# One-element additions that tie a graph layer's turning of finished rows to a later source tile

## Chip, cores and metric

The kernel runs on one NeuronCore of a Trainium2 chip. TensorE (PE in the profile) does matrix products and transposes, VectorE (DVE) and ScalarE (ACT) elementwise work, GpSimd (POOL) slower elementwise work and indirect transfers, SyncE (SP) issues transfers. Each engine works through its own list of instructions in a fixed order, and waits at an instruction until the semaphores that it names have been raised. The metric is the device time of one execution in microseconds; lower is better. Three runs of the kernel before took 1935.4, 1935.51 and 1937.74 us, so the median is 1935.51 us.

## What is computed

Four layers over 3125 nodes with 256 features: a three-layer graph attention network, an expert layer with 16 experts of which each node takes two, a graph sum layer, and an expert layer with 8 experts of which each node takes one. The change touches the first of these. Cut to it, the reference is:

```python
def _gat_layer(x, src, dst, W, al, ar, b, n_nodes):
    h = x @ W
    el = h @ al
    er = h @ ar
    e = jax.nn.leaky_relu(el[src] + er[dst], NEG_SLOPE)
    m = jax.ops.segment_max(e, dst, num_segments=n_nodes)
    ex = jnp.exp(e - m[dst])
    s = jax.ops.segment_sum(ex, dst, num_segments=n_nodes)
    alpha = ex / s[dst]
    out = jax.ops.segment_sum(alpha[:, None] * h[src], dst, num_segments=n_nodes)
    return out + b
...
h = jax.nn.relu(_gat_layer(x, src, dst, W1, al1, ar1, b1, n))
h = jax.nn.relu(_gat_layer(h, src, dst, W2, al2, ar2, b2, n))
h = _gat_layer(h, src, dst, W3, al3, ar3, b3, n)
```

There are 103,125 edges, loops included.

## The kernel before

The attention layers are computed densely. The kernel counts the edges between every pair of nodes once, during the first layer, into a matrix of small numbers (`counts`). A layer is then a product: for destination nodes d and source nodes s, the weight of s for d is a count times the larger of two exponential terms, and the sum over s is a matrix product on TensorE. With a column of ones scaled like the rest carried as column 257 of the source rows, the same product gives the softmax's denominator.

The work is tiled in 128 nodes: 25 tiles, the last with 53 nodes. Two destination tiles make a group, so that there are 13 groups, the last with one tile of 53. The loops are: three layers (`i`), in each 13 groups (`a`), in each 25 source tiles (`s`). For each group:

- line 1228: TensorE transposes the group's destination scores, and ACT (line 1230) makes `tau` of them;
- for each `s`, VectorE makes the factors `pm` (line 1247: the larger of `tau` and a source value, times the counts; six buffers), and TensorE multiplies them with the source rows (line 1250) into `acc`, a pair of PSUM banks, one for each tile of the group; each product in this precision is two passes on the array;
- when all 25 are summed, the group is finished in steps that are put in a list `later` and called at stated values of `s` of the next group.

The steps for the first and the second layer are `divide` (called at s = 8, or 6 after the last full group), in which VectorE computes the denominators' reciprocals `col` (lines 1268 and 1269) and the finished rows `y` (line 1277, one instruction for each tile of the group), and `onward`, called at s = 10 for the first tile and s = 13 for the second. `onward` turns the finished rows: two transposes on TensorE (line 1290) into a PSUM tile `ps_m`, a ReLU copy on ACT into `yT` (line 1292), and then `put` of the next layer's sources: the product with the next weights (line 1098, again in `ps_m`), a clamp on VectorE (line 1101) and three ACT instructions (lines 1102 to 1105). `ps_m` has two buffers, which the transposes of line 1228 use too. The third layer has no `onward`; its groups go on to the router.

During the first layer TensorE also counts edges for the next group: `counter.make` prepares one-hot matrices on VectorE (line 1581) and ACT (lines 1577 and 1578), `counter.add` multiplies them (line 1593, six products a pair of windows, into `acc_c`, of which there are two buffers) and ACT casts the result into `counts` (line 1596).

The order of instructions on each engine isn't the order of the program text. A scheduler lays the instructions out by priority, which follows the text, and by when it reckons their inputs to be ready. A transposition whose input it reckons to be ready early may stand earlier than its place in the text: in the second layer, the transposes of a group's first finished tile stand directly after those of line 1228, ahead of the next group's products; in the first layer one of the two stands there from group 3 on.

Of the kernel before, what the change touches and what calls it, by code (L numbers as in the profile page):

```python
# [16 lines left out]
OP = mybir.AluOpType  # L17
# [1021 lines left out]
def attention_weights(tc, cp, one, layers, i, behind=None):  # L1039


    nc = tc.nc
    w, al, ar, b = layers[i]
    we = cp.tile([P, KD, D + 2], F32, name="we")
    at = cp.tile([P, 2, D], F32, name="wa")
    bt = cp.tile([P, D], F32, name="wb")
    if behind is not None:
        for to in (we[:, 0], at[:, 0], at[:, 1], bt):
            nc.gpsimd.tensor_copy(to[:, 0:1], behind)
    nc.sync.dma_start(at[:, 0], spread(al, D))  # L1050
    nc.sync.dma_start(at[:, 1], spread(ar, D))
    nc.sync.dma_start(we[:, :, :D], w.rearrange("(k p) f -> p k f", p=P))

    def products(behind=None):
        nc.sync.dma_start(bt, spread(b, D))
        junk = one.tile([P, D], F32, name="wjunk")
        if behind is not None:
            nc.vector.tensor_copy(junk[:, 0:1], behind)
        for k in range(KD):
            for j in range(2):  # L1060
                nc.vector.scalar_tensor_tensor(junk, we[:, k, :D], 1.0, at[:, j], op0=OP.mult, op1=OP.mult,
                                               accum_out=we[:, k, D + j:D + j + 1])
    return we, bt, products
# [8 lines left out]
def block(big, d=D):  # L1072

    return big.tile([P, NT * (D + 1)], F32, name="big")[:, :NT * d].rearrange("p (t d) -> p t d", d=d)
# [33 lines left out]
def dense_attention(tc, dram, counts, x_in, big, ident, eps, layers, src, dst, rows, high, make_router, over):  # L1108
# [9 lines left out]
    nc = tc.nc  # L1118
    with tc.tile_pool(name="dw", bufs=1) as cp, tc.tile_pool(name="dwl", bufs=2) as wl, \
# [10 lines left out]
        with tc.tile_pool(name="dp", bufs=6) as pmp, tc.tile_pool(name="ds", bufs=2) as sp, \  # L1130
# [70 lines left out]

            third = ExitStack()
            later = []
            fills = []
            for i in range(3):
                last = i == 2
                bt_i = bt
                if last:
                    wp = third.enter_context(tc.tile_pool(name="ro", bufs=2))
                    rp = third.enter_context(tc.tile_pool(name="ror", bufs=4))  # L1210
                    zp = third.enter_context(tc.tile_pool(name="rop", bufs=1, space=PSUM))
                    router = make_router(third.enter_context(tc.tile_pool(name="roc", bufs=1)))
                    y_out = block(big)
                    nc.gpsimd.memset(y_out[:, NT - 1], 0.0)
                    nxt, we_n = None, None
                else:
                    nxt = Sources(tc, big, small)
                    we_n, bt, products = attention_weights(tc, wl, cp, layers, i + 1, now.rho[:, NT - 1:])
                    products()
                for a, (c, n) in enumerate(GROUPS):  # L1220
                    tiles = [(q, (c + q) // P, min(P, n - q)) for q in range(0, n, P)]

                    edges = counts_of(counts, a)
                    ahead = list(pairs[a + 1]) if i == 0 and a + 1 < len(GROUPS) else []
                    ready = []
                    ps = pp.tile([P, PAIR], F32, name="ps_m")
                    for q, t, r in tiles:
                        nc.tensor.transpose(ps[:, q:q + P], now.lr[:, 1, t:t + 1].to_broadcast([P, P]), ident)  # L1228
                    tau = sp.tile([P, PAIR], F32, name="tau")
                    nc.scalar.activation(tau[:, :n], ps[:, :n], AF.Exp, scale=-0.8)  # L1230
                    acc = ap_.tile([P, 2, CHUNK], F32, name="acc")
                    rest = []
                    if last:
                        for q, t, r in tiles:
                            xi = sp.tile([P, D], F32, name=f"y{q // P}")
                            nc.sync.dma_start(xi[:r], x_in[t * P:t * P + r])
                            nc.gpsimd.tensor_tensor(xi[:r], xi[:r], bt_i[:r], op=OP.add)
                            rest.append(xi)
                    for s in range(NT):
                        if i == 0 and s == 16 and a in (1, 3, 5):  # L1240
                            locator.finish((a + 1) // 2, pp)
                        if i == 0 and (a, s) in FIND:
                            locator.find(FIND.index((a, s)) + 1, kp, tau[:, 0:1])
                        while later and later[0][0] == s:
                            later.pop(0)[1]()
                        pm = pmp.tile([P, PAIR], F32, name="pm")
                        nc.vector.scalar_tensor_tensor(pm[:, :n], tau[:, :n], now.rho[:, s:s + 1],  # L1247
                                                       edges[:, s, :n], op0=OP.max, op1=OP.mult)
                        for j, (q, t, r) in enumerate(tiles):
                            nc.tensor.matmul(acc[:r, j, :D + 1], pm[:, q:q + r], now.h[:, s], start=(s == 0),  # L1250
                                             stop=(s == NT - 1))
                        for pair in ready:
                            counter.add(kp, pair)
                        if s == 2 and fills:

                            for e in empties:
                                nc.gpsimd.tensor_scalar(e, tau[:, 0:1], 0.0, None, op0=OP.mult)
                        if s % 8 == 2 and fills:
                            fills.pop(0)()
                        ready = [ahead.pop(0) for _ in range(-(-len(ahead) // max(1, NT - 1 - s)))]  # L1260
                        for pair in ready:
                            counter.make(pair, ACT_OH, tau[:, 0:1] if a == 0 and s < 5 else None)

                    def divide(tiles=tiles, acc=acc, rest=rest, b=bt_i, last=last):

                        col = sp.tile([P, 2], F32, name="col")
                        nt, r0 = len(tiles), tiles[0][2]
                        nc.vector.tensor_scalar(col[:r0, :nt], acc[:r0, :nt, D], 1e-30, None, op0=OP.max)
                        nc.vector.reciprocal(col[:r0, :nt], col[:r0, :nt])
                        for j, (q, t, r) in enumerate(tiles):  # L1270
                            if last:
                                to, add = y_out[:r, t], rest[j][:r]
                            else:
                                y = sp.tile([P, D], F32, name=f"y{j}")
                                rest.append(y)
                                to, add = y[:r], b[:r]
                            nc.vector.scalar_tensor_tensor(to, acc[:r, j, :D], col[:r, j:j + 1], add, op0=OP.mult,
                                                           op1=OP.add)


                    sooner = 2 if a == len(GROUPS) - 2 else 0
                    later.append((8 - sooner, divide))
                    if last:
                        norm, gate, send = router.group(wp, rp, zp, y_out, tiles[0][1], len(tiles))
                        later += [(9 - sooner, norm), (11 - sooner, gate), (14 - sooner, send)]
                    for j, (q, t, r) in enumerate(tiles if not last else []):
                        def onward(j=j, t=t, r=r, rest=rest, nxt=nxt, w=we_n):
                            ps = pp.tile([P, KD, P], F32, name="ps_m")
                            for k in range(KD):
                                nc.tensor.transpose(ps[:, k, :r], rest[j][:r, k * P:(k + 1) * P], ident[:r, :r])  # L1290
                            yT = sp.tile([P, KD, P], F32, name=f"yT{j}")
                            nc.scalar.activation(yT[:, :, :r], ps[:, :, :r], AF.Relu)
                            nxt.put(pp, t, r, [yT[:, :, :r]], w)
                        later.append((10 + 3 * j, onward))
                    if i == 0 and a == 1:
                        fills, empties = spare_rows(tc, cp, *rows)
                if i == 0:
                    first.close()
                nc.vector.tensor_reduce(top[:, i:i + 1], now.lr, AX.XY, OP.max, apply_absolute_value=True)
                now = nxt  # L1300
# [441 lines left out]
```

## Time and profile before

| | |
|---|---|
| median of three runs | 1935.51 us (1935.4 to 1937.74) |
| the profiled execution's own time | 1939.77 us |
| its span, first to last instruction | 1938.0 us |
| mean granted TensorE clock over the span | 0.986 |
| first layer, groups 0 to 12, TensorE's products (line 1250) | 68.1 to 489.3 us of the span |
| second layer | 490.7 to 807.3 us |
| third layer | 808.6 to 1107.8 us |
| one full group of the first layer (347.71 to 381.43) | 33.72 us |
| one full group of the second layer (565.80 to 591.09) | 25.29 us |
| transposes of line 1290 | 100, mean 276 ns |
| finished rows of line 1277, first two layers | 50, median 479 ns |

How to read the profile: a line of the list of groups names the line of the kernel, the engine, the operation, what it writes and reads, the shape and the count; after the bar come the busy time in us and the mean of one in ns, and after the second bar the idle time of the engine just before such instructions, with what ended it. In the timeline each row has the start in us from the span's start, the duration in us, and the engine; in square brackets stands the idle time before it and what ended that. TensorE has two rows of instructions: PE for the products and PEld for the loading of the stationary operand, which overlaps the products. Products are pipelined, so that the start of the next is a better measure of what one costs than its own duration.

### The profile page before, as it was taken

The page shows a single profiled execution, that of the slowest core. Times are in us where ns is not written, and L with a number is a line of the kernel's source. Part 1 is how long each engine was busy: PE and PEld are TensorE (multiplying, and loading weights), DVE is VectorE, ACT ScalarE, POOL GpSimd, SP SyncE. Part 2 cuts the span into 40 slices and gives each one's busy share as a digit, 9 for nine tenths or more (in the row PEclk, how much of TensorE's full clock was granted, in tenths as well). Part 3 has the DMA queues.
Part 4 walks back from the last instruction along what each step waited for, and adds up shares of the span by engine and source line. Part 5 has one row for each costly group of instructions (what it writes and reads, how often), then busy time and mean ns, then how long its engine had stood idle before and what let it go on. Part 6 is the DMA issues. An engine that isn't in the chain of part 4 may idle for free. (4 is left out here: it accounts for less than half of the span.)

```text
span 1938.0 us, 27811 instructions
## 1 busy us (share of the span) xinstructions
PE 1847.1 (95%) x9386; PEld 1470.1 (76%) x9386; DVE 1001.0 (52%) x2909; ACT 748.3 (39%) x2252; POOL 295.8 (15%) x453
## 2 busy tenths in 40 slices
PE   6999999999999999999999979999979999997998
PEld 4788888887788888788888657777658887554887
DVE  6889888785555555567777622222234222323122
ACT  4767777672010001122222211111127999544221
POOL 4200000000000000023333322233310000132122
PEclk9999999999999999999999989999989999999999
DMA  4101123575100000011111155668540000633764
GB/s 124 32 12 62 41 66 120 207 282 237 55 1 1 1 1 3 9 56 44 44 44 44 63 176 150 187 177 243 128 94 1 1 1 1 228 156 125 211 208 138
DMA packets 103577, 182.96 MB, mean 94 GB/s; under 512 B 10054, under 2 KB 72741, under 8 KB 103392
## 3 DMA queue, kind: packets, MB, share of 16 engines
q1 hardware_dynamic: 72268, 124.32, 19.1%
q0 software_dynamic: 16016, 34.28, 6.5%
q10 hardware_dynamic: 15138, 22.44, 3.7%
q8 instruction: 80, 1.31, 0.3%
q14 instruction: 75, 0.61, 0.1%
HBM read 92.93 MB, written 90.17 MB: 94 GB/s over the span
## 5 line engine op out<-in xcount | busy, mean ns | idle before, releaser
L1250 PE MATMUL acc<-big,pm 128*128 128x257 f32 (+1 forms) x3750 | 871.9, 383 | 5.2 <-DVE pm L1247 4.9
L1250 PEld LDWEIGHTS acc<-big,pm 128*128 128x128 f32 (+1 forms) x3750 | 681.2, 187 | 111.4 <-DVE pm L1247 10.1
L1247 DVE SCALAR_TENSOR_TENSOR pm<-tau,rho,counts 128x256 f32<-128x256 f32 (+1 forms) x975 | 435.9, 466 | 160.3 <-PE acc L1250 157.6
L754 PE MATMUL ps_h<-xsT,w 128*128 128x384 f32 x512 | 169.6, 490 | 0.4 <-ACT xsT L730 0.4
L1369 PE MATMUL acc<-msg,cr 128*128 128x512 f32 (+1 forms) x625 | 157.8, 403 | 0.1
L1581 DVE TENSOR_TENSOR ohk<-iota_k,key 128x1200 f16<-128x1200 f16 x196 | 151.6, 774 | 5.5 <-PE acc_c L1593 5.4
L754 PEld LDWEIGHTS ps_h<-xsT,w 128*128 128x128 f32 x512 | 98.1, 192 | 66.0 <-issue 1.5
L1369 PEld LDWEIGHTS acc<-msg,cr 128*128 128x128 f32 (+1 forms) x625 | 114.7, 185 | 29.2 <-ACT cr L1365 1.2
L1365 ACT ACTIVATE cr<-counts 128x256 fp32r<-128x256 uint8 (+1 forms) x325 | 130.5, 402 | 14.6 <-DMA sums<-y,who 6.8
L1593 PE MATMUL acc_c<-ohk,ohs 128*128 128x200 f16 x1176 | 130.7, 250 | 0.6 <-ACT ohs L1578 0.6
L1577 ACT ACTIVATE far<-iota_s,low 128x128 f16<-128x128 f16 x360 | 123.5, 397 | 6.1 <-POOL far L1575 1.8
L1593 PEld LDWEIGHTS <-ohs 128*128 128x128 f16 x1176 | 105.3, 98 | 25.8 <-ACT ohs L1578 1.0
L982 PE MATMUL ps_y<-t_wd,hsT 128*128 x480 | 109.6, 382 | 0.0
L757 ACT ACTIVATE silu<-ps_h 128x384 f32<-128x384 f32 x64 | 31.4, 490 | 201.4 <-PE ps_h L754 199.3
L758 DVE TENSOR_TENSOR hid<-silu,ps_h 128x384 f32<-128x384 f32 x64 | 35.4, 554 | 140.6 <-PE ps_h L754 127.6
L1596 ACT CAST counts<-acc_c 128x400 uint8<-128x400 f32 x196 | 93.1, 479 | 34.6 <-PE acc_c L1593 33.8
L982 PEld LDWEIGHTS ps_y<-t_wd,hsT 128*128 128x128 f32 x480 | 89.4, 191 | 11.3 <-ACT hsT L1010 0.3
L1230 ACT ACTIVATE tau<-ps_m 128x256 f32<-128x256 f32 (+1 forms) x39 | 14.1, 369 | 215.5 <-PE ps_m L1228 197.4
L772 POOL DMA_INDIRECT sums<-y,who x48 | 74.9, 1561 | 131.2 <-DVE y L770 106.8
L890 PE MATMUL ps_H<-big,t_w 128*128 128x512 f32 (+1 forms) x224 | 93.1, 552 | 0.7 <-ACT H L892 0.5
L767 PE MATMUL ps_o<-w,hid 128*128 128x256 f32 x384 | 86.9, 379 | 0.0
L1581 DVE TENSOR_TENSOR ohs<-iota_s,low 128x512 f16<-128x512 f16 (+1 forms) x196 | 83.4, 426 | 0.0
(289 smaller groups left out, 1895.3 us busy)
## 6 DMA issues: line engine op xcount, KB each, us to landing
rows<-empty SPq DMA_DIRECT2D x16, 2564.0 KB
w<-in_L_ffn_w_dram ACTq DMA_DIRECT2D x42, 512.0 KB
hs<-rows SPq DMA_DIRECT2D x29, 641.0 KB
w<-in_L_ffn_w_dram SPq DMA_DIRECT2D x30, 512.0 KB
rows<-empty SPq DMA_DIRECT2D x16, 516.0 KB
t_wd<-in_L_ffn_Wd_dram SPq DMA_DIRECT2D x8, 1024.0 KB
xs<-rows SPq DMA_DIRECT2D x15, 387.0 KB
bias<-in_L_ffn_bd_dram SPq DMA_DIRECT2D x30, 128.0 KB
```

What stands on the lines that cost most here:

```text
L754: nc.tensor.matmul(ps, w[:, k, j * P:(j + 1) * P], xsT[:, k], start=(k == 0), stop=(k == KD - 1))
L767: nc.tensor.matmul(ps, hid[:, j, q * P:(q + 1) * P], o[:, j], start=(j == 0), stop=(j == nh - 1))
L890: nc.tensor.matmul(ps[:, :n], a[:, k, j * P:(j + 1) * P], xnT[:, k, c:c + n], start=(k == 0), stop=(k == KD - 1))
L982: nc.tensor.matmul(ps, hsT[:, j], d[:, ds(e, 1), j, :].rearrange("p o f -> p (o f)"), start=(j == 0), stop=(j == nh - 1))
L1247: nc.vector.scalar_tensor_tensor(pm[:, :n], tau[:, :n], now.rho[:, s:s + 1], edges[:, s, :n], op0=OP.max, op1=OP.mult)
L1250: nc.tensor.matmul(acc[:r, j, :D + 1], pm[:, q:q + r], now.h[:, s], start=(s == 0), stop=(s == NT - 1))
L1365: nc.scalar.activation(cr[:, :n], edges[:, s, :n], AF.Copy, accum_out=seen[:, a * NT + s:a * NT + s + 1])
L1369: nc.tensor.matmul(acc[:r, j].rearrange("p h d -> p (h d)"), cr[:, q:q + r], msg[:, s].rearrange("p h d -> p (h d)"), start=(s == 0), stop ...
L1577: nc.scalar.activation(far[:, i], self.iota_s, AF.Abs, scale=-1.0, bias=self.low32[:, pair, i:i + 1])
L1581: nc.vector.tensor_tensor(to[:, i:].rearrange("p t (x u) -> p t x u", u=2), iota.rearrange("p (x u) -> p x u", u=2)[:, None].to_broadcast( ...
L1593: nc.tensor.matmul(acc[:, u], ohs[:, i], ohk[:, i], start=(t == 0), stop=(t == TW - 1))
L1596: nc.scalar.copy(to[:, :, d0 % PAIR:d0 % PAIR + 2 * WIN].rearrange("p s (u d) -> p u s d", u=2), acc.rearrange("p u (s d) -> p u s d", d=WIN))
```

## The change

Every `onward` of the first two layers now begins with one instruction on VectorE: it multiplies one element of the factors `pm` that were made last before the call by zero, and adds it to the first element of the finished tile, which it writes in place. The value is unchanged. The transposes of that tile read the result, so they come after this addition, and the addition comes after the factors of source tile s - 1, that is 9 for the first tile of a group and 12 for the second.

```diff
             third = ExitStack()
             later = []
+            pms = []
...
                         pm = pmp.tile([P, PAIR], F32, name="pm")
+                        pms.append(pm)
...
                         def onward(j=j, t=t, r=r, rest=rest, nxt=nxt, w=we_n):
+
+                            nc.vector.scalar_tensor_tensor(rest[j][0:1, 0:1], pms[-1][0:1, 0:1], 0.0, rest[j][0:1, 0:1],
+                                                           op0=OP.mult, op1=OP.add)
                             ps = pp.tile([P, KD, P], F32, name="ps_m")
                             for k in range(KD):
                                 nc.tensor.transpose(ps[:, k, :r], rest[j][:r, k * P:(k + 1) * P], ident[:r, :r])
```

There are 25 such calls for each of the two layers, 50 in all.

## The prediction

> **What bounds the kernel now.** I read the page first, then who waits for whom around the moved transposes, then the instructions in order of time at one head of a group, and at one place inside a group.
>
> ```profile
> span 1938.0 us, 27811 instructions
> PE 1847.1 (95%) x9386; PEld 1470.1 (76%) x9386; DVE 1001.0 (52%) x2909; ACT 748.3 (39%) x2252; POOL 295.8 (15%) x453
> ...
> L1250 PE MATMUL acc<-big,pm 128*128 128x257 f32 (+1 forms) x3750 | 871.9, 383 | 5.2 <-DVE pm L1247 4.9
> ...
> L1247 DVE SCALAR_TENSOR_TENSOR pm<-tau,rho,counts 128x256 f32<-128x256 f32 (+1 forms) x975 | 435.9, 466 | 160.3 <-PE acc L1250 157.6
> ```
>
> TensorE is the bound: the products of the three graph layers run without a break but for 5.2 us, while VectorE, which makes their factors pm, sat 157.6 us waiting for TensorE to give buffers back. So TensorE's time counts everywhere in this stage, VectorE's only where TensorE stands at a head (the start of a group of destination tiles). The transposes of line 1290 in the second layer and the start of the third:
>
> ```profile
> its engine sat idle before it (us, times) until:
>   ACT tau L1230: 12.3, 12
>   DVE y L1277: 10.6, 13
> ```
>
> These are 13 heads with some 0.8 us each (the two rows are the weight queue's and the matmul queue's view of the same stand). It looks like 10.6 us to be had by moving the transposes away. One head shows what they stand in:
>
> ```profile
> 564.27 0.38 PE L1228 MATMUL ps_m<-ident,lr 128*128 128x128 f32 x2
> ...
> 564.69 0.38 ACT L1230 ACTIVATE tau<-ps_m 128x256 f32<-128x256 f32 x1 [8.86 <-PE ps_m L1228]
> 564.87 0.48 DVE L1277 SCALAR_TENSOR_TENSOR y<-acc,col,wb 128x256 f32<-128x256 f32 x1
> 565.27 0.48 DVE L1247 SCALAR_TENSOR_TENSOR pm<-tau,rho,counts 128x256 f32<-128x256 f32 x1
> 565.47 0.20 PEld L1290 LDWEIGHTS ps_m<-ident,y 128*128 128x128 f32 x2 [1.05 <-ACT tau L1230]
> 565.50 0.41 PE L1290 MATMUL ps_m<-ident,y 128*128 128x128 f32 x2 [0.84 <-DVE y L1277]
> ```
>
> The next moment, in the same view:
>
> ```profile
> 565.80 0.30 PEld L1250 LDWEIGHTS acc<-big,pm 128*128 128x128 f32 x2
> 565.80 0.48 PE L1250 MATMUL acc<-big,pm 128*128 128x257 f32 x1
> ```
>
> The group's first pm runs from 565.27 to 565.75, and the first load of it into TensorE starts at 565.80, 0.05 us later. The transposes' own loads started 0.12 us after their y was done (564.87 + 0.48 = 565.35), so 0.05 is no more than a hand-over. The head is therefore ended by pm, not by the transposes: these run from 565.47 to their last start at 565.61, inside a stand that lasts until pm is there anyway.
>
> **The change, part by part.** It removes nothing. It adds 50 additions of one element on VectorE (25 tiles, two layers), and in the built order of the changed kernel every transpose of a first tile y0 now stands between the products of source tiles 9 and 10, as y1 already stands between 12 and 13. The heads keep their order otherwise: col, reciprocal, y, then the first pm on VectorE. No DMA is moved, and the queues of SP and POOL keep their order.
>
> *Second layer, 11 full heads and what they lose.* At the head nothing is gained: pm still ends the stand. Inside the group the two transposes cost TensorE their own time. y1, already there, gives the price:
>
> ```profile
> 578.06 0.38 PE L1290 MATMUL ps_m<-ident,y 128*128 128x128 f32 x2
> ...
> 578.28 0.38 PE L1250 MATMUL acc<-big,pm 128*128 128x257 f32 x1
> ```
>
> 578.28 - 578.06 = 0.22 us for a pair without any stand. 11 x 0.22 = +2.4 us. The product that follows (line 1098) needs yT from ACT; for y1 it comes after four passes, just in time, and y0 gets the same four.
>
> *Two odd heads.* The last tile of a layer (53 nodes) is turned in group 0 of the second and of the third layer. Between products of 128 columns a load of 53 columns breaks the pipeline: at 817.50 the step into the 53-column products of line 1098 took 0.31 us and the step out again 0.31, where two full products are 0.22 apart; the two small transposes themselves are 0.08 apart (808.31 and 808.38). That makes 0.31 + 0.08 + 0.31 - 0.22 = 0.48 us each, +1.0 us. At least they cost their 0.15 each (+0.3).
>
> *First layer, 9 heads.* There only one of the two transposes stood at the head, after twelve products of the edge counting:
>
> ```profile
> 346.40 1.19 PE L1593 MATMUL acc_c<-ohk,ohs 128*128 128x200 f16 x12
> ...
> 347.12 0.49 ACT L1596 CAST counts<-acc_c 128x400 uint8<-128x400 f32 x1
> 347.18 0.47 DVE L1247 SCALAR_TENSOR_TENSOR pm<-tau,rho,counts 128x256 f32<-128x256 f32 x1
> ...
> 347.43 0.27 PE L1290 MATMUL ps_m<-ident,y 128*128 128x128 f32 x1
> ```
>
> ```profile
> 347.71 0.19 PEld L1250 LDWEIGHTS acc<-big,pm 128*128 128x128 f32 x1 [0.22 <-DVE pm L1247]
> ```
>
> In the changed order a thirteenth counting product takes the transpose's place at the head. Later the group has one counting product less (0.09, as 1.19 - 0.25 over 11 steps) and one transpose more (0.11, half of 0.22): +0.02. The thirteenth needs a buffer acc_c that the cast at 347.12 frees at 347.61; with 0.05 of hand-over and its own 0.09 TensorE is at 347.75, against 347.71 now: +0.04. Bounds of this wait: 0, if the load of pm still starts at 347.71, and 0.74, if the buffer were that of the next cast (347.82 to 348.31 in the timeline, + 0.05 + 0.09 - 347.71). I take 0.04, as the buffers alternate by two. 9 x 0.06 = +0.5 us (0.2 to 6.8). The early groups, where the edge finder's work stands at the head, are put at nothing, give or take 0.5.
>
> *The additions.* The nearest row is a column operation, col, 0.16 us and the next start 0.19 after it; waiting for the pm just issued adds some 0.1 (pm starts 0.40 apart, and lasts 0.48). So about 0.3 us each, 15 us in all, if nothing hid them. What hides them is VectorE's stand of 0.38 us before each pm, which is the 157.6 us above; pm runs up to six tiles ahead. Behind an addition stand the next pm and behind that the product; in the timeline pm number 10 is done 4.5 us (second layer) and 2.2 us (first) before its product starts, so 0.3 is covered: 0, with +15 as the other end.
>
> Sum: 2.4 + 1.0 + 0.5 = +3.9 us. On the profiled execution (1939.77 us, of which the span is 1938.0 and 1.8 lie around it) this is 1943.7; that execution is 4.3 over the median of the runs, and I predict from the median: 1935.51 + 3.9 = 1939.4 us.
>
> *Rules of the skill.* The stand at a head is now unbroken, 1.4 us, from 564.38 to 565.80. The granted clock over the second layer, with 1.1 us stands already in it:
>
> ```profile
> 490.00:808.00 318.00, 307.34 (x1425) 258.93 (x1425) 161.34 (x403) 32.06 (x114) 3.96 (x7) 1.00 0.01 3
> ```
>
> It is 1.00. The Trainium skill, "TensorE: Matmul & The Clock Gate", section "What's actually happening", says that an idle window of about 3.4 us halves the clock; that rule would speak against longer stands, at an estimated 1.7 us for each of 13 heads (22 us), but 1.4 us doesn't reach the window, and by row and rule the sum stays. The same page, section "Back-to-back issue gap", would give a transpose of 128 columns 56 ns, and the 11 full pairs an estimated 1.2 us instead of 2.4; the row of 0.22 for a pair decides.
>
> **The rivals.** *The stand at the heads goes (faster).* If the first product had waited for the transposes and not for pm, the 10.6 us of line 1290 would be saved and the 3.4 us inside the groups paid: 1935.5 - 10.6 + 3.4 = 1928.3. For it: the size of that row. Against it: pm done at 565.75 and loaded at 565.80. It decides where pm is done more than 0.14 us before the load, the time of the pair at the head; in the heads I looked at in both layers the distance is 0.05.
>
> *The thirteenth counting product holds the head (clearly slower).* With the bound of 0.74 the first layer costs 6.8: 2.4 + 1.0 + 6.8 = 10.2, or 1945.7. For it: in the changed order this product waits for ACT, directly ahead of the group's first product. Against it: the cast that frees its buffer ends before pm does (347.61 and 347.65).
>
> *Nothing moves in time (no change).* If the odd heads cost 0.3, the counting swap 0, and hand-overs hide part of the pairs, 2 us or less are left, 1937.5 and under; or the additions fail to hold anything, 1935.5. Against the last: the order has the transposes inside the groups.
>
> **How the numbers follow.** The forecast, +2.4 to +5.5, has 0.76; the held head 0.10; the vanished stand 0.06; no effect 0.08. Below 0.2% (3.9 us, about what a measurement of this kernel can tell from no change) lies a bit less than half of the forecast. Faster 0.06, same 0.42, slower 0.52. The range goes from 1937.2, which leaves out the two lower rivals (0.14), to 1943.5, above the forecast's 1941 towards the held head.
>
> **What would show it.** Right: at a head of the second layer pm ends and TensorE's first load starts 0.05 us later, with a stand of 1.4 us put down to pm of line 1247 instead of y; a group lasts 25.5 us there instead of 25.29; the additions show no waiter but the transposes. Wrong: a group of 25.0 us or less (the stand went), or of the first layer with 34 us and more instead of 33.72, with line 1593 waiting for ACT, or idle time before pm or before line 1290 inside the groups (additions too late).

## The result and the profile after

The changed kernel took 1942.03 us (median of 10 runs, 1938.34 to 1944.91) beside 1936.81 us for the kernel before (10 runs, 1935.4 to 1938.73); the ratio is 1.0021, 95% interval [1.0013, 1.003]. Measured a second time beside other runs of the kernel before, it was 1940.66 us against 1937.16 and 1.0017 [1.0008, 1.0026]. The medians lie 5.2 us apart in the first measurement, while the two ratios stand for 4.1 and 3.3 us and the trace, as shown below, for 3.2; so the change costs some 3 to 4 us, about 0.2%. The profiled execution took 1939.52 us, with a span of 1937.8 us. Line numbers of the changed kernel are higher by 2 around pm and y and by 5 behind the addition: tau 1231, col 1270, reciprocal 1271, pm 1249, products 1252, y 1279, addition 1291, transposes 1295, yT 1297.

The page of the changed kernel, with its busy row and the groups of the products (behind the first bar busy time and mean ns of one, behind the second the idle time before them and what ended most of it):

```profile
span 1937.8 us, 27658 instructions
...
PE 1845.3 (95%) x9386; PEld 1469.6 (76%) x9386; DVE 1007.0 (52%) x2959; ACT 746.9 (39%) x2252; POOL 294.7 (15%) x453
...
L1252 PE MATMUL acc<-big,pm 128*128 128x257 f32 (+1 forms) x3750 | 873.1, 382 | 18.6 <-DVE pm L1249 18.4
...
L1249 DVE SCALAR_TENSOR_TENSOR pm<-tau,rho,counts 128x256 f32<-128x256 f32 (+1 forms) x975 | 436.4, 467 | 155.8 <-PE acc L1252 153.0
```

VectorE has 50 instructions more, and TensorE's products now stood 18.6 us for pm, where it was 5.2. That is not 13 us of new loss. In the kernel before, the same stands were put down to y at line 1290 (10.6 us there), because the transposes were the first thing behind the stand. Who waited around the transposes now:

```profile
L1295 PE MATMUL ps_m<-ident,y x100: 222/273/329, 117.1 to 818.5; 128*128 128x128 f32 x96, 53*128 53x53 f32 x4
...
its engine sat idle before it (us, times) until:
  issue: 2.3, 6
```

No wait for tau or y is left at the transposes. One head of the second layer in order of time (start, busy time, engine, line and tiles, and in brackets the idle time before it and what ended it):

```profile
563.23 0.38 PE L1229 MATMUL ps_m<-ident,lr 128*128 128x128 f32 x2
...
563.64 0.38 ACT L1231 ACTIVATE tau<-ps_m 128x256 f32<-128x256 f32 x1 [8.86 <-PE ps_m L1229]
563.82 0.48 DVE L1279 SCALAR_TENSOR_TENSOR y<-acc,col,wb 128x256 f32<-128x256 f32 x1
564.22 1.27 DVE L1249 SCALAR_TENSOR_TENSOR pm<-tau,rho,counts 128x256 f32<-128x256 f32 x3
564.75 0.73 PEld L1252 LDWEIGHTS acc<-big,pm 128*128 128x128 f32 x4 [1.39 <-DVE pm L1249]
564.75 0.92 PE L1252 MATMUL acc<-big,pm 128*128 128x257 f32 x3 [1.15 <-DVE pm L1249]
```

The three pm of 1.27 us begin at 564.22, which is 0.40 us after y and without idle time of VectorE before them; tau had been ready since 563.64 + 0.38 = 564.02. So pm waits for its turn on VectorE behind col, reciprocal and y, and not for tau. It is the same at the 11 full heads of the second layer, before and after the change: pm starts 0.40 us behind y and 0.13 to 0.20 us after the end of tau. At 0.48 us the first ends at 564.70, and its load starts at 564.75. From the tau transposes to the first product it is 564.75 - 563.23 = 1.52 us, and it was 565.80 - 564.27 = 1.53: the head is as long without the transposes as with them. Their new place, in the same group:

```profile
573.54 0.38 PE L1295 MATMUL ps_m<-ident,y 128*128 128x128 f32 x2
573.76 1.03 PE L1252 MATMUL acc<-big,pm 128*128 128x257 f32 x4
574.63 0.60 PE L1098 MATMUL ps_m<-we,yT 128*128 128x258 f32 x2
```

573.76 - 573.54 = 0.22 us that nothing hides; line 1098 follows without a stand after four passes, 574.63 - 573.76 = 0.87 us.

Where the time went is read best from the start of each group's first product. In the table, "group 1st" and "group 2nd" are the distance of two such starts in the first and second layer (full groups, late in the layer), "second layer" is from its first product to the third layer's first, and "third, first group" is the distance to the next group's start. The later rows are the experiments; all of these are single profiles, worked out from the trace's starts, in us.

| kernel | ratio to before [95%] | group 1st | group 2nd | second layer | third, first group |
|---|---|---|---|---|---|
| before | | 33.72 | 25.29 | 317.94 | 24.60 |
| changed | 1.0021 [1.0013, 1.003] | 33.65 | 25.51 | 320.81 | 25.41 |
| after_again | 1.0017 [1.0008, 1.0026] | 33.65 | 25.51 | 320.81 | 25.41 |
| scrap | 0.9995 [0.9986, 1.0004] | 33.66 | 25.29 | 317.95 | 24.95 |
| hold_first | 0.9994 [0.9986, 1.0003] | 33.65 | 25.29 | 318.41 | 24.60 |
| hold_second | 1.0013 [1.0004, 1.0022] | 33.72 | 25.51 | 320.37 | 25.05 |
| hold_y1 | 0.9999 [0.999, 1.0008] | 33.78 | 25.29 | 317.95 | 24.60 |
| double_mid | 1.0044 [1.0032, 1.0056] | 33.96 | 25.73 | 323.42 | 25.06 |
| double_head | 1.0016 [1.0006, 1.0026] | 33.93 | 25.35 | 318.84 | 24.60 |
| tau_ahead | 0.9902 [0.9886, 0.9919] | 33.17 | 24.10 | 304.15 | 23.23 |
| tau_ahead_hold | 0.9903 [0.9886, 0.9919] | 33.17 | 24.10 | 304.60 | 23.68 |

From the start of the fourth group to the last product of the third layer the changed kernel took 933.49 us (175.68 to 1109.17) and its repetition 933.50, the kernel before 930.32 (177.07 to 1107.39): +3.2 us, 0.16%, which agrees with both ratios. What comes before the fourth group can't be put down to the change: two profiles of the changed kernel itself reached it at 175.68 and 176.85 us.

### The profile page after: what moved, and what is told of

Read it like the earlier page. It is cut to its first block, busy times and chain, and to the rows that moved or that the text cites. A ratio compares the mean times of both kernels' runs of the same rounds, so it can differ in the third digit from the quotient of the medians.

```text
span 1937.8 us, 27658 instructions
## 1 busy us (share of the span) xinstructions
PE 1845.3 (95%) x9386; PEld 1469.6 (76%) x9386; DVE 1007.0 (52%) x2959; ACT 746.9 (39%) x2252; POOL 294.7 (15%) x453
## 5 line engine op out<-in xcount | busy, mean ns | idle before, releaser
L1252 PE MATMUL acc<-big,pm 128*128 128x257 f32 (+1 forms) x3750 | 873.1, 382 | 18.6 <-DVE pm L1249 18.4
```

## The experiments

The theory: the head is ended by pm, so the transposes there cost nothing, and in the middle of a group they cost their own 0.22 us. Against it stood that the additions cost VectorE time, that the first layer or something outside the graph layers carries part of the loss, and that the finished rows end the head. All kernels here keep the line numbers of the kernel before.

**Additions that hold nothing (scrap).**

```diff
-nc.vector.scalar_tensor_tensor(rest[j][0:1, 0:1], pms[-1][0:1, 0:1], 0.0, rest[j][0:1, 0:1],
-                               op0=OP.mult, op1=OP.add)
+scrap = sp.tile([1, 1], F32, name="scrap")
+nc.vector.scalar_tensor_tensor(scrap, pms[-1][0:1, 0:1], 0.0, rest[j][0:1, 0:1],
+                               op0=OP.mult, op1=OP.add)
```

> The 50 additions are kept with what they read (the tile's row and the last factors), but write to a one-element tile that nobody uses, so that they hold nothing and the transposes of y0 stay at the heads in the built order. If the cost is that of the transposes' new place, a group of the second layer lasts 25.29 us as before, the second layer 317.9 us from its first product to the third layer's first (before 317.9, after 320.8), and the run is within 0.1% of the kernel before. If the additions themselves cost VectorE time that reaches the products, the second layer lasts 320.8 us although the transposes stay, and the run is some 0.2% slower.

Measured: 1936.46 us against 1937.15, ratio 0.9995 [0.9986, 1.0004]; a group of the second layer 25.29 us, the layer 317.95. The 50 additions cost nothing that these runs can measure. In the changed kernel one of the second layer looks like this:

```profile
568.33 1.46 PE L1252 MATMUL acc<-big,pm 128*128 128x257 f32 x6
...
568.53 0.48 DVE L1249 SCALAR_TENSOR_TENSOR pm<-tau,rho,counts 128x256 f32<-128x256 f32 x1 [0.28 <-PE acc L1252]
569.05 0.15 DVE L1291 SCALAR_TENSOR_TENSOR y<-pm,y 1x1 f32<-1x1 f32 x1
569.40 0.48 DVE L1249 SCALAR_TENSOR_TENSOR pm<-tau,rho,counts 128x256 f32<-128x256 f32 x1 [0.20 <-PE acc L1252]
```

It lasts 0.15 us and lies in the pause in which VectorE waits for TensorE anyway: the pm behind it still waits 0.20 us for a buffer.

**Only the second tile held (hold_y1).** The addition is made only where j == 1; the transposes of y1 stand between source tiles 12 and 13 with or without it.

> Only the second tile y1 of a group is held, 24 additions. Its transposes stand between source tiles 12 and 13 with or without the hold, so my theory expects nothing: a full group of the second layer 25.29 us, the second layer 317.9 us, and a run within 0.1% of the kernel before. If the additions delay pm or the transposes behind them, the second layer grows by 0.1 us or more for each of its 12 groups.

Measured: 1936.51 against 1937.16, ratio 0.9999 [0.999, 1.0008]; 25.29 us a group. In the second layer the second tile's part of the change neither costs nor brings anything. In the first layer a group is 33.78 us long, 0.06 more than before, which was not expected and is taken up below.

**One layer at a time (hold_first, hold_second).** The addition is made only for i == 0, or only for i == 1.

> The rows are held in the first layer alone. My theory (the transposes' own time in the open) expects a full group of the first layer of 33.66 us as in the changed kernel, the head of the second layer's first group 0.44 us dearer (its 53-node tile belongs to the first layer), full groups of the second layer of 25.29 us, so 318.4 us for the second layer, and a run 1 to 1.5 us below the kernel before. The rival, that the part of the difference of the medians which the pair of profiles does not show (4 to 5 us against 1.8 us at the end of the graph layers) comes from the first layer, expects a run 1 to 2 us above.

Measured: 1936.7 against 1937.15, ratio 0.9994 [0.9986, 1.0003], which is -1.2 us (-2.7 to +0.6). Groups of 33.65 and 25.29 us, and the second layer 318.41 us: the +0.46 of its first group, the first of the two odd heads, and nothing else. The interval speaks against the rival's 1 to 2 us above, but it holds both zero and the 1 to 1.5 us below that were expected. The trace shows no difference: from the fourth group's start to the third layer's last product 930.31 us, against 930.32 before, since the first layer's gain of 0.56 us and the odd head's cost of 0.46 us nearly cancel. That the ratio fell on the expected value is chance.

> The rows are held in the second layer alone. My theory expects the first layer as before (a full group 33.72 us), full groups of the second layer of 25.51 us, the second layer 11 x 0.22 = 2.4 us longer than before (320.4 us), the first group of the third layer 0.46 us longer (23.63 us), and so a run 2.9 us (0.15%) above the kernel before. If the cost came from the additions in both layers alike, half of it would be here.

Measured: 1939.68 against 1937.15, ratio 1.0013 [1.0004, 1.0022], +2.5 us; 25.51 us a group, and the layer 320.37 us, 2.43 longer, for 2.4 expected. The third layer's first group is 25.05 - 24.60 = 0.45 us longer, the other odd head; the 23.63 us in the expectation started from a length that this group doesn't have in the kernel before, 24.60. The loss sits in the layer where the transposes moved off a stand; additions alone, in both layers, cost nothing (scrap).

**The pair done twice in its new place (double_mid), and twice at the head (double_head).** The first is the changed kernel, the second the kernel before, both with

```diff
-for k in range(KD):
+for k in 2 * [*range(KD)] if j == 0 and r == P else range(KD):
     nc.tensor.transpose(ps[:, k, :r], rest[j][:r, k * P:(k + 1) * P], ident[:r, :r])
```

> The changed kernel with the pair of transposes of a full first tile y0 done twice, where it now stands, between the products of source tiles 9 and 10, in both layers. If the change costs the transposes' own time, each second pair costs 0.22 us again: a full group of the second layer lasts 25.73 us and the second layer 320.8 + 12 x 0.22 = 323.4 us; the first layer has the same 0.22 us more for each of its 10 full groups with such a pair, some 2 us, so the run is about 5 us above the changed kernel. If the cost of 0.22 us were a hand-over (the wait for y0 or for yT) and not the transposes' time, the group would stay at 25.51 us.

Measured: 1945.88 against 1937.15, ratio 1.0044 [1.0032, 1.0056]; 25.73 us a group of the second layer and 323.42 us for that layer, both as expected. In the first layer a group got 0.31 us longer (33.65 to 33.96) where 0.22 was expected; the other 0.09 is a longer step into a product of line 1098, 0.32 us instead of 0.23. The four transposes in a group of the second layer:

```profile
576.97 0.60 PE L1290 MATMUL ps_m<-ident,y 128*128 128x128 f32 x4
577.40 1.03 PE L1250 MATMUL acc<-big,pm 128*128 128x257 f32 x4
```

0.43 us for four, 0.11 for each: in the second layer it is the transposes' own time, and no hand-over. The section "Back-to-back issue gap" of the Trainium skill's "TensorE: Matmul & The Clock Gate" gives about 56 ns for an isolated matmul of 128 columns and about 81 ns in a sustained stream, without telling data types apart. By these figures a group would have been an estimated 25.62 or 25.67 us long; the measured 25.73 decides.

> The kernel before, with the pair of transposes of a full first tile y0 done twice. In the second layer both pairs stand at the head in the built order, so this asks how much the stand still hides. My theory says that the first product waits for pm, done at 565.75 us in the head shown, and that four transposes from 565.47 us, 0.11 us apart, end at 565.91 us: 0.1 us longer than the pm chain, so a full group of the second layer lasts 25.40 us (25.29 before, and 25.51 if the second pair were not hidden at all, 25.29 if there were more room than I think). In the first layer, where the second pair lands between the products, a full group gets 0.22 us longer.

Measured: 1940.85 against 1937.28, ratio 1.0016 [1.0006, 1.0026], most of it from the first layer (33.93 us a group); in the second layer a group is 25.35 us (25.40 expected), +0.06 for the same second pair that costs 0.22 in the middle. Its head:

```profile
567.21 0.38 PE L1228 MATMUL ps_m<-ident,lr 128*128 128x128 f32 x2
...
568.21 1.66 DVE L1247 SCALAR_TENSOR_TENSOR pm<-tau,rho,counts 128x256 f32<-128x256 f32 x4
...
568.44 0.63 PE L1290 MATMUL ps_m<-ident,y 128*128 128x128 f32 x4 [0.85 <-DVE y L1277]
568.80 0.95 PEld L1250 LDWEIGHTS acc<-big,pm 128*128 128x128 f32 x5
568.91 1.03 PE L1250 MATMUL acc<-big,pm 128*128 128x257 f32 x4
```

pm is done at 568.69, and now the load no longer follows it by 0.05 but comes at 568.80, behind the four transposes. The stand is 568.91 - 567.21 = 1.70 us instead of 1.53; 0.11 of it comes back, because the first load now runs 0.11 us ahead of its product instead of at the same moment: the step from the first product to the second is 0.22 us here, and 0.32 at the heads of the kernel before. So the stand hid 0.16 of the second pair's 0.22 us as well, and with four transposes its room is used up.

**The stand itself taken away (tau_ahead, tau_ahead_hold).** tau of the next group is made inside the group before it, at source tile 18; in the second kernel the rows are held as in the changed kernel as well.

```diff
-ps = pp.tile([P, PAIR], F32, name="ps_m")
-for q, t, r in tiles:
-    nc.tensor.transpose(ps[:, q:q + P], now.lr[:, 1, t:t + 1].to_broadcast([P, P]), ident)
-tau = sp.tile([P, PAIR], F32, name="tau")
-nc.scalar.activation(tau[:, :n], ps[:, :n], AF.Exp, scale=-0.8)
+def limits(a, c, n, now=now):
...
+if a == 0:
+    taus = {}
+    limits(a, c, n)
+tau = taus[a]
+if a + 1 < len(GROUPS):
+    later.append((18, lambda a=a, limits=limits: limits(a + 1, *GROUPS[a + 1])))
```

Here limits holds the five lines taken out, and puts its tile into taus[a].

> The kernel before with the factors' limit tau of a group made in the group before it, at source tile 18, instead of at its head; nothing is held. In the built order the first six pm of a group then stand ahead of col and y on VectorE, and the transposes of y0 stand behind source tile 8 by themselves. If a head is ended by pm, as I say, and not by y0 and its transposes, the stand goes: a full group of the second layer loses the 1.53 us from the tau transposes' start to the first product and gains two pairs in the open, 2 x 0.22 us, so 25.29 - 1.09 = 24.20 us and some 12.5 us for the layer; the third layer has only three such heads, about 2 us; the first layer fills its heads with counting products, 0 to 3 us. In all 1937.2 - 16 = 1921 us (1918 to 1924). The rival, that the head is ended by the finished rows (col, reciprocal, y0, transposes), keeps a stand of some 1 us at each head: a group of 25 us or more.

Measured: 1919.52 us against 1937.28, ratio 0.9902 [0.9886, 0.9919], 19 us less: faster than both kernels. A group of the second layer is 24.10 us long (24.20 expected, and 25 or more by the rival). The 0.10 us beyond the expectation is the longer first step behind a stand (0.32 us instead of 0.22), which goes with the stand. That layer gave 13.8 us (12.5 expected); the first gave 3.9 from its fourth group on, where 0 to 3 was expected, and the third 0.5 where 2 was. The border between two groups, with the next group's first product at 580.29 us:

```profile
577.26 4.93 PE L1250 MATMUL acc<-big,pm 128*128 128x257 f32 x22
...
580.89 0.15 DVE L1268 TENSOR_SCALAR col<-acc 128x2 f32<-128x2 f32 x1
581.08 0.17 DVE L1269 RECIPROCAL col<-col 128x2 f32<-128x2 f32 x1
581.28 0.48 DVE L1277 SCALAR_TENSOR_TENSOR y<-acc,col,wb 128x256 f32<-128x256 f32 x1
```

22 passes run across the border without a break, and the finishing of the rows begins 0.6 us after it, off the path. Two things have changed here at once: tau is ready early, and the first pm of a group stand ahead of col, reciprocal and y on VectorE. At the heads of the kernel before, tau was ready 0.13 to 0.20 us before pm began, so an earlier tau behind the same order of VectorE would have brought nothing, and pm ahead of col and y but behind the late tau an estimated 0.2 us a head at most. Neither was run by itself. The rival of the expectation is out only in so far as it means the transposes or y as what the first product waits for; that VectorE's work on the finished rows makes pm late is what the heads show. Over the second layer TensorE was busy for 303.45 of 304.15 us (columns: window, its length, then busy time and instructions of PE, PEld, DVE, ACT and POOL, the granted clock, the DMA share and GB/s):

```profile
484.76:788.91 304.15, 303.45 (x1425) 258.43 (x1425) 167.92 (x403) 31.94 (x113) 3.27 (x7) 1.00 0.01 3
```

> As the kernel with tau made ahead, and with the rows held as in the changed kernel. The transposes of full tiles stand inside the groups in both, so my theory gives the hold nothing to gain: the same 24.20 us for a full group of the second layer, and the two 53-node tiles moved off their heads at 0.45 us each, so about 0.9 us above the kernel with tau made ahead alone. If the hold were useful once pm no longer ends the heads, this would be the faster of the two.

Measured: 1919.81 us, ratio 0.9903 [0.9886, 0.9919]. The groups are the same 24.10 us, and the two odd heads are dearer by 0.45 us each (304.60 and 23.68), as expected; the medians, 0.3 us apart, can't tell 0.9 us, while the traces show it (913.15 against 912.24 us from the fourth group's start to the third layer's last product). The hold brings nothing here either, since the transposes of full tiles stand inside the groups in both kernels.

**The whole once more (after_again).**

> The changed kernel once more, with the edit put on lines that were there. Hold_first gave 0.06% less and hold_second 0.13% more than the kernel before; if the whole is their sum and nothing else, it is 0.07%, or 1.4 us; the starts of the layers give +2.9 us in the second layer, 0.5 us in the third layer's first group and -0.6 us in the first, 2.8 us or 0.14%; the first measurement of the whole gave 0.21% (0.13 to 0.30). I expect 0.10% to 0.20%, that is 1939 to 1941 us; 0.25% or more would mean that something outside the graph layers costs time too.

Measured: 1940.66 us, ratio 1.0017 [1.0008, 1.0026]. Nothing outside the graph layers is needed to explain the difference.

## Why the prediction was right, and where it wasn't

*The head is ended by pm: shown.* The stand is as long without the transposes (1.52 us) as with them (1.53), a second pair of transposes there costs 0.06 of its 0.22 us (double_head), and the stand goes when pm comes earlier (tau_ahead). The prediction stopped at pm and didn't ask what makes pm late; by the trace it is col, reciprocal and y ahead of it on VectorE, which begins pm 0.13 to 0.20 us after tau is ready. (The second transpose of the head shown starts at 565.63 by its trace, and not at 565.61 as the prediction has it; nothing rests on that.) The rival that the stand would go with the transposes, which rested on the 10.6 us before line 1290, is out: that row named the last release before the first thing queued, not what the products waited for.

*Second layer, 0.22 us for each of 11 pairs: shown,* to the hundredth (25.51 instead of 25.29; hold_second +2.43; double_mid 0.22 again).

*Odd heads, 0.48 us each: shown,* 0.46 and 0.45 measured.

*Additions at nothing: shown* by scrap, and for the second layer by hold_y1. The size put on one, about 0.3 us, is not confirmed: after 20 of the 50, all in the first layer, the next pm starts 0.07 us after the addition's start, and in the second layer mostly 0.35 us, of which 0.20 is pm's own wait for a buffer.

*First layer, +0.06 us a group: the sign was wrong.* The step that failed was to take the head and the swapped counting product for all that moves there. Steps of TensorE in one full group, summed by what comes next, worked out from the starts in the two traces (the group that begins at 381.43 us before and at 379.62 us in the changed kernel):

```
                                   before    changed
between counting products,
  transposes and what follows       8.848      8.903     +0.055
into line 1098 (waits for yT)       1.038      0.946     -0.092
between products of pm             18.850     18.815     -0.035
everything else                     4.990      4.989
group                              33.726     33.653     -0.073
```

The swap and the thirteenth product's wait for ACT came out at +0.055, as predicted (0.06). What was left out is that a product of line 1098 had been standing 0.12 us for yT in each group (a step of 0.341 us at 361.35, where full products are 0.217 apart). Before the change, TensorE and ACT, each from a view of its own:

```profile
360.25 0.27 PE L1290 MATMUL ps_m<-ident,y 128*128 128x128 f32 x1
360.35 1.03 PE L1250 MATMUL acc<-big,pm 128*128 128x257 f32 x4
361.35 0.70 PE L1098 MATMUL ps_m<-we,yT 128*128 128x258 f32 x2
```

```profile
360.91 0.38 ACT L1292 ACTIVATE yT<-ps_m 128x256 f32<-128x256 f32 x1
```

And in the changed kernel:

```profile
358.38 0.38 PE L1295 MATMUL ps_m<-ident,y 128*128 128x128 f32 x2
358.60 1.03 PE L1252 MATMUL acc<-big,pm 128*128 128x257 f32 x4
359.48 0.70 PE L1098 MATMUL ps_m<-we,yT 128*128 128x258 f32 x2
```

```profile
359.04 0.38 ACT L1297 ACTIVATE yT<-ps_m 128x256 f32<-128x256 f32 x1
```

yT starts 0.66 us after the first start of line 1290 here in both kernels. With the second transpose in the stream the four products start 0.12 us later beside it, and line 1098 finds yT ready. So the moved transpose, 0.11 us, fills a stand that was there; its time is hidden in this layer, where the prediction added it. The other product of line 1098 waits 0.02 us more. The steps between products of pm are 0.035 us shorter in sum, which these runs don't explain.

This layer also moves when no transpose does. In scrap, whose transposes stay where they were, a group is 33.66 us long, and in hold_y1, with its transposes in the same places, 33.78. The difference lies at the group's second wait for yT: the step into line 1098 there is 0.70 us before, 0.63 in scrap and 0.76 in hold_y1. So one-element additions alone shift this layer by -0.07 to +0.06 us a group, and the predicted term of 0.06 is no larger than that. The held-head rival (0.74 us a group) is out: the group got no longer.

*The sum.* By the layers: -0.54 in the first (fourth to last group, 313.61 to 313.07 us), +2.87 in the second, +0.81 in the third's first group: +3.2 us with the rounding, where 3.9 was predicted. The third's 0.81 is 0.46 for the odd head and 0.35 for a pause that wasn't foreseen (below). The first layer came out 1.0 us lower than predicted and the third 0.35 higher, so the misses partly cancel. The measured 1942.03 us is 2.6 above the predicted 1939.4; 1.3 of that is the kernel before, whose median in these runs was 1936.81 and not the 1935.51 that the prediction started from. The other 1.3 is the 5.2 us between the medians against the 3.9 predicted; the traces show 3.2, so no term of the sum stands behind it.

*The longer unbroken stand and the clock.* The stand of 1.4 us at each head didn't lower the granted clock; over the second layer of the changed kernel it is 1.00 as before:

```profile
488.75:809.55 320.80, 306.59 (x1425) 258.57 (x1425) 165.16 (x428) 32.01 (x113) 3.08 (x7) 1.00 0.01 3
```

The section "What's actually happening" of the same page of the skill puts the window of idleness at about 3.4 us; these runs agree with it from below, and none has a stand in this layer that reaches it.

## What to carry to other kernels

Work on the bounding engine that lies inside a stand ended by something else is free there. Moved into the open it costs its full time (0.22 us a pair in the second layer), unless it falls into another stand (the first layer). So before moving it, find what is done last at the stand (here pm, 0.05 us before the load) rather than what the idle row names, and then what makes that late (here col, reciprocal and y, ahead of pm on VectorE). The gain lay in that chain: with tau made a group earlier and pm ahead of the finishing of the rows, 19 us went, while moving what was hidden in the stand added 3 to 4. And in a scheduled kernel, list all waits that the new order touches, the ones that may vanish too.

## What the runs showed that wasn't expected

VectorE paused without a releaser that explains it, between the reciprocal and y of a head of the third layer. In the changed kernel:

```profile
833.41 0.17 DVE L1271 RECIPROCAL col<-col 128x2 f32<-128x2 f32 x1
834.03 0.48 DVE L1279 SCALAR_TENSOR_TENSOR big<-acc,col,y 128x256 f32<-128x256 f32 x1 [0.46 <-DVE col L1271]
```

The step is 0.62 us, where it was 0.27 at the same head of the kernel before (832.02 to 832.29). The same instruction, number 1448 of VectorE's in the trace, paused in both profiles of the changed kernel and in scrap, and there it delays the first pm by 0.35 us. In double_mid, with 50 additions as well but another order of VectorE's instructions, that head has no pause, and a later one has it (934.20 to 934.82). In hold_second one of 0.32 us stands in the router's work (898.26), and the third layer's fourth group lasts 23.75 us there instead of 23.39. The kernel before has such a pause as well, at another head, where the first pm had been made before and the group's products run on:

```profile
1047.94 0.17 DVE L1269 RECIPROCAL col<-col 128x2 f32<-128x2 f32 x1
1048.57 0.48 DVE L1277 SCALAR_TENSOR_TENSOR big<-acc,col,y 128x256 f32<-128x256 f32 x1 [0.46 <-issue]
```

In the two profiles of the changed kernel, whose VectorE instructions are the same, it came in the same place; where their order or number differs it stood elsewhere, or between no reciprocal and y at all. So the 0.35 us that it adds to the changed kernel is no price of the transposes' new place. Its cause isn't shown by these runs.
